# A four-layer graph network on one core: first transfers spread over three queues, constants behind them, two layers started beside the one before, one copy given priority

## The chip, the cores and the metric

The kernel runs on one core of one Trainium2 chip. The metric is the time of one execution in device microseconds (us); lower is better. Engines in the profile: PE is TensorE's matmul, DVE is VectorE, ACT is ScalarE, POOL is GpSimd, SP is SyncE, which here only issues transfers.

## The reference, cut to what matters

128 graphs of 64 nodes with 256 features go through four residual layers, each followed by a layer normalisation.

```python
# layer 0: five fixed groups of nodes, a two-step graph convolution each, mixed by softmax(fusion_w)
A = adj_g + eye;  dinv = deg(A) ** -0.5;  norm = dinv * A * dinv.T
h = relu(norm @ (x_g @ W1[g]) + b1[g]);   o = relu(norm @ (h @ W2[g]) + b2[g])
x = layernorm(x + scatter_add(softmax(fusion_w)[g] * o))
# layer 1: one graph convolution with the whole adjacency;  layer 2: a cubic in adj / rowsum, leaky relu
x = layernorm(x + norm(adj) @ (x @ W) + b)
x = layernorm(x + leaky(sum_k conv_w[k] * (adj/rowsum)**k @ (x @ W.T) + conv_b))
# layer 3: five GRU steps over messages from the neighbours
for l in range(5):
    h = gru_cell((adj != 0) @ (h @ weight[l]), h)
x = layernorm(x + h * mask)
```

All arithmetic is float32. The kernel does layer 0 in 8 batches of 16 graphs, layers 1 and 2 and the GRU in 16 chunks of 8 graphs.

## The kernel before

Layer 0 works through its batches with generators: `prep` makes the scaled adjacency of the next batch, `groups` multiplies this one, `residual` adds and normalises the last. Each engine gets its instructions in a fixed order. For TensorE in the later part that is the program's order; for the others a scheduler decides when the program is built.

```python
def load0(s):                        # one batch: 18 adjacency pieces, 12 x pieces, two whole x chunks
    ...
    nc.sync.dma_start(a0[s % 2][rows, t, col : col + m], adj[b, f : f + n, fc : fc + m])
    ...
    nc.sync.dma_start(xg[rows, t, :], x[b, f : f + n, :])
    ...
loaded = {0: load0(0)}
ident = const(c_ident, [128, 128], "ident", nc.scalar)
...
for g in range(NG):                  # ten weights of 512 KB
    nc.scalar.dma_start(W1[:, g], ...)
    nc.gpsimd.dma_start(W2[:, g], ...)
b2c = const(...);  fw = spread(fusion_w, NG, "fw", w0)
fm = ... ; fe = exp(...) ; gw = softmax ; gb2 = b2c * gw     # a chain over VectorE and ScalarE

def prep(s):
    nc.vector.tensor_add(ae, a, eye0)
    nc.vector.tensor_reduce(deg, ae, AX.X, ALU.add)
    dinv = inv_sqrt(deg, NT, TR, "d0")        # the power runs on GpSimd: d0s -> d0r -> d0o
    ...
    nc.tensor.transpose(p[:, t, :], A0[:, t0 + t, :], ident[:TR, :TR])
    nc.vector.tensor_mul(AT[:, t0 : t0 + n, :], p, dinv...)
    ...
for s in range(NS):                           # layer 0
    ...
    interleave(*beside, groups(s))
interleave(residual(NS - 1))                  # stores x1[c] to DRAM

loaded = {0: load(0), 1: load(1)}             # reloads x1 and the whole adjacency of two chunks
... # constants of layers 1 and 2
    interleave(both(mid(0), mid(1)), fold())  # layers 1 and 2 of two chunks, beside folding the GRU weights

def turn(self, k):                            # GRU: new state, transposed, copied for the next messages
    p = self.transpose(...)
    if not last:
        nc.scalar.copy(self.h[:, :, f], pv)
    ...
```

## Time and profile before

| what | before |
|---|---|
| time, median of 3 runs | 2423.56 us (2421.87 to 2425.59) |
| TensorE busy | 2270.2 us, 94% |
| to the first matmul | 38.68 us |
| batches 0 and 1, to batch 2's transposes | 67.08 us |
| from there to batch 7's transposes | 202.16 us |
| from there to the first GRU product | 176.79 us |
| GRU | 1939.89 us |

The last five rows cut the profiled run of 2424.6 us where the same work starts, so that they can be laid beside any other version. The page and the stretches are shown in the prediction below. One place that it mentions without showing is the start of layers 1 and 2 (TensorE's timeline: start, length, engine, line, operation, out<-in, shapes, count, then the idle time before it and what ended it):

```profile
396.51 1.09 PE L535 MATMUL pT<-ident,A 128*128 128x128 f32 x4 [19.78 <-DVE d1z L89]
...
404.45 3.78 PE L496 MATMUL pa<-AT,xt 128*128 128x128 f32 x16 [6.00 <-DVE AT L536]
```

TensorE stood still for 19.78 us and then, after eight transposes, for 6.00 more.

### The profile page before, as it was taken

The numbers are of one execution on the slowest core, as the hardware profiler recorded it, in microseconds if no ns is written. First come the engines' busy times: TensorE is split into PE (matmuls) and PEld (weight loads), VectorE is DVE, ScalarE is ACT, GpSimd is POOL, SyncE is SP. The second block draws the span as 40 slices with busy tenths as digits, with TensorE's granted clock in tenths as the row PEclk, the third lists the DMA queues.
The fourth block names the chain that finished last, engine by engine and source line by source line (L and its number), as shares of the span: only waits on it lengthen the run. The fifth ranks groups of instructions, "written<-read, shape, count | busy, mean of one in ns | idle before, by whom it ended". The sixth has DMA issues, their size and how long they took to land.

```text
span 2424.6 us, 31697 instructions
## 1 busy us (share of the span) xinstructions
PE 2270.2 (94%) x12288; PEld 2001.0 (83%) x12288; DVE 1324.7 (55%) x2914; ACT 1094.5 (45%) x2102; POOL 569.4 (23%) x606
## 2 busy tenths in 40 slices
PE   3999994899999999999999999999999999999996
PEld 2778783788888888888888888888888888888885
DVE  1334324555566556655666566656665566556556
ACT  1343441445454545454445444444544454445443
POOL 1101002222222322222222213222322232223221
PEclk9999997999999999999999999999999999999998
DMA  5232113000001000100010001000100000000000
GB/s 152 67 86 85 50 53 117 3 3 1 3 6 33 1 3 1 38 1 3 1 38 1 3 1 38 1 3 1 36 2 1 1 27 1 1 1 18 1 1 18
DMA packets 55319, 54.34 MB, mean 22 GB/s; under 512 B 24225, under 2 KB 48513, under 8 KB 55169
## 3 DMA queue, kind: packets, MB, share of 16 engines
q1 hardware_dynamic: 51616, 43.74, 5.8%
q0 software_dynamic: 1504, 5.51, 0.7%
q10 hardware_dynamic: 2048, 3.06, 0.4%
q8 instruction: 97, 1.59, 0.3%
q14 instruction: 54, 0.43, 0.1%
HBM read 35.52 MB, written 16.78 MB: 22 GB/s over the span
## 4 chain that ended last, share of the span: by engine, by line
PE 78%; DVE 13%; ACT 4%; DMA 2%; issue 2%; POOL 1%; SPq 1%; POOLq 0%; ACTq 0%; DVEq 0%
PE parz L460 19%; PE pan L460 9%; PE pdrz L460 9%; PE pa L496 8%; PE ps L289 5%; PE pdn L460 5%; PE pbrz L460 5%; PE ph L274 4%; PE pT L596 3%; PE pbn L460 3%; PE pd L575 2%; ACT xt L113 2%; DMA a<-in_adj_dram 2%; PE pp L550 1%; DVE st L102 1%
## 5 line engine op out<-in xcount | busy, mean ns | idle before, releaser
L476 ACT COPY c<-parz 128x512 f32<-128x512 f32 x240 | 140.4, 585 | 362.7 <-PE parz L460 362.7
L460 PE MATMUL parz<-Th,WHH 128*128 128x256 f32 x960 | 285.9, 379 | 0.0
L460 PE MATMUL parz<-Ta,V 128*128 128x256 f32 x960 | 285.5, 379 | 0.0
L440 POOL TENSOR_TENSOR Th<-hn 128x512 f32<-128x512 f32 x64 | 93.5, 1461 | 659.7 <-DVE hn L656 659.7
L653 ACT ACTIVATE NI<-NI,bih 128x512 f32<-128x512 f32 x160 | 115.5, 722 | 227.0 <-DVE NI L649 227.0
L460 PEld LDWEIGHTS parz<-Ta,V 128*128 128x128 f32 x960 | 182.4, 190 | 24.8
L476 ACT COPY c<-pan 128x512 f32<-128x512 f32 x240 | 140.8, 586 | 122.2 <-PE pan L460 122.2
L460 PEld LDWEIGHTS parz<-Th,WHH 128*128 128x128 f32 x960 | 176.0, 190 | 21.2 <-ACT c L476 0.5
L440 POOL TENSOR_TENSOR Ta<-agg 128x512 f32<-128x512 f32 x80 | 101.6, 1270 | 369.9 <-ACT agg L499 369.9
L488 DVE TENSOR_TENSOR RZ<-pdrz,c 128x512 f32<-128x512 f32 x80 | 55.2, 690 | 223.0 <-PE pdrz L460 223.0
L626 ACT ACTIVATE RZ<-RZ,brz 128x512 f32<-128x512 f32 x160 | 106.9, 716 | 121.3 <-DVE RZ L488 121.3
L107 POOL TENSOR_TENSOR rs<-ve,mhalf 128x4 f32<-128x4 f32 x64 | 64.6, 1010 | 408.6 <-DVE ve L105 396.3
L496 PEld LDWEIGHTS pa<-A,h 128*128 128x128 f32 x1024 | 128.1, 198 | 33.0 <-ACT h L669 30.4
L496 PE MATMUL pa<-A,h 128*128 128x128 f32 x1024 | 131.6, 284 | 24.8 <-ACT h L669 24.8
L460 PE MATMUL pan<-Ta,V 128*128 128x256 f32 x480 | 143.2, 380 | 3.1 <-ACT c L476 3.1
L482 DVE TENSOR_TENSOR NI<-pbn,c 128x512 f32<-128x512 f32 x80 | 55.3, 691 | 164.0 <-PE pbn L460 163.9
L460 PE MATMUL pan<-Th,WHH 128*128 128x256 f32 x480 | 142.8, 379 | 0.0
L289 PE MATMUL ps<-W,hg 128*100 128x256 f32 (+3 forms) x576 | 133.2, 384 | 0.0
L113 ACT ACTIVATE xt<-xt,nb,rs 128x256 f32<-128x256 f32 x192 | 99.6, 589 | 43.9 <-DVE nb L110 43.6
L289 PEld LDWEIGHTS ps<-W,hg 128*100 128x100 f32 (+3 forms) x576 | 91.8, 164 | 27.8
L478 DVE TENSOR_TENSOR NI<-pdn,c 128x512 f32<-128x512 f32 x80 | 54.8, 684 | 104.8 <-ACT c L476 104.8
L655 DVE TENSOR_TENSOR RZ<-RZ 128x512 f32<-128x512 f32 x160 | 109.8, 686 | 2.3
(183 smaller groups left out, 5241.1 us busy)
## 6 DMA issues: line engine op xcount, KB each, us to landing
xt<-in_x_dram SPq DMA_DIRECT2D x16, 512.0 KB
x<-xt SPq DMA_DIRECT2D x16, 512.0 KB
xt<-x SPq DMA_DIRECT2D x16, 512.0 KB
out_dram<-xt SPq DMA_DIRECT2D x16, 512.0 KB
xg<-in_x_dram SPq DMA_DIRECT2D x32, 100.0 KB
W<-in_w_dram POOLq DMA_DIRECT2D x5, 512.0 KB, 9.2
W<-in_w_dram ACTq DMA_DIRECT2D x5, 512.0 KB
a<-in_adj_dram SPq DMA_DIRECT2D x16, 128.0 KB
```

The lines of the kernel that those rows point to most:

```text
L107: nc.gpsimd.tensor_tensor(rs, ve, mhalf[:, :NP], ALU.pow)
L113: nc.scalar.activation(y[:, p, :], y[:, p, :], AF.Identity, bias=nb[:, p : p + 1], scale=rs[:, p : p + 1])
L274: nc.tensor.matmul(p, W1[:, g, k, e * 128 : (e + 1) * 128], ag0[:, k, o : o + w], start=k == 0, stop=k == 1)
L289: nc.tensor.matmul(p[:r, h, :], hg[:, e, TOFF[t] - o : TOFF[t] - o + r], W2[:, g, e, :], start=e == 0, stop=e == 3,)
L440: nc.gpsimd.tensor_sub(t[:, 0:2, :], a[:, :, H:], a[:, 0, :].rearrange("p (s n) -> p s n", s=2))
L460: nc.tensor.matmul(bank[:, g, :], w[:, q, i - 1, :], rhs, start=i in (1, 2, 5) and g == 0 and m == 0, stop=m == len(side) - 1, skip_group_ ...
L476: nc.scalar.copy(c, self.a)
L496: nc.tensor.matmul(p[:, q * 128 : (q + 1) * 128], src[:, q, k * 128 : (k + 1) * 128], m[:, q, :], start=True, stop=True)
L596: nc.tensor.transpose(p[:, q * 128 : (q + 1) * 128], src(q, k), ident)
L626: nc.scalar.activation(RZ[:, q, 0, :], RZ[:, q, 0, :], AF.Sigmoid, bias=b[0])
L653: nc.scalar.activation(n, n, AF.Tanh, bias=bih[:, 4 + j : 5 + j])
L655: nc.vector.tensor_mul(d, d, z)
```

## The change

The intent is to fill TensorE's idle stretches: get the first batches' data in first, load what the middle needs during layer 0, give TensorE two chunks of layers 1 and 2 beside layer 0's last batch, and let the copy that the GRU's messages wait for pass other work on ScalarE. The diff, cut to its core (moved code and names are left out, and the pools: layer 0's eight PSUM buffers, a pool of its own before, are now shared with the later layers, as five and three, and the tiles of layers 1 and 2 no longer come from a pool opened after layer 0):

```diff
 def load0(s):
+    qa = [nc.scalar, nc.sync] if s == 0 else [nc.sync]      # adjacency pieces
+    qx = nc.gpsimd if s < 2 else nc.sync                     # x pieces
...
-loaded = {0: load0(0)}
-ident, eye0, block0, b1 on ScalarE;  W1 on ScalarE, W2 on GpSimd;  b2, fw on SyncE
+eye0 = const(c_eye0, [TR, NT, NJ], "eye0", nc.scalar, w0)
+packed = {0: load0(0)}
+ident, block0, b1 on ScalarE;  W1, W2 on SyncE
+packed[1] = load0(1)
+xts = {0: load_x(0)}
+b2c = const(..., "b2", nc.scalar, w0)
+fw = spread(fusion_w, NG, "fw", w0, nc.scalar)
...
 for s in range(NS):
-        beside.append(prep(s + 1))
+        beside.append(prep(s + 1) if s else both(range(6), prep(s + 1)))   # batch 1: six steps later
+    if s == 1:          # constants of layers 1 and 2, on GpSimd behind its latest power
+    elif s == 3:        # GRU weights, the same way
+    elif s == NS - 1:
+        for c in (0, 1):
+            loaded[c] = load(c)
+        beside.append(both(mid(0), mid(1)))
     interleave(*beside, groups(s))
...
-    interleave(both(mid(0), mid(1)), fold())
+    weights = fold()    # now in three parts, around the two chunks' states and messages
...
     if not last:
-        nc.scalar.copy(self.h[:, :, f], pv)
+        with tc.high_priority():
+            nc.scalar.copy(self.h[:, :, f], pv)
```

## The prediction

> **What bounds the kernel now.** I read the page's first part, then the busy time by stretch, the chain of waits at the start and in the middle, TensorE's timeline at both, and last who TensorE waits for in the long GRU part.
>
> ```profile
> PE 2270.2 (94%) x12288; PEld 2001.0 (83%) x12288; DVE 1324.7 (55%) x2914; ACT 1094.5 (45%) x2102; POOL 569.4 (23%) x606
> ...
> PE   3999994899999999999999999999999999999996
> ```
>
> TensorE is the bound at 94%; VectorE is next at 55%. So the time can fall only where a slice of TensorE isn't 9: the first, slices 7 and 8, and the last, which is the tail of the final chunk. Cutting the run at the program's stages (columns: start:end, length, then PE busy with its count and the other engines', granted clock, DMA share, GB/s):
>
> ```profile
> 0.00:38.60 38.60, 0.00 (x0) 0.00 (x0) 2.84 (x11) 0.00 (x0) 8.63 (x12) 1.00 0.66 198
> 38.60:97.50 58.90, 52.46 (x286) 44.10 (x287) 12.80 (x53) 20.58 (x46) 3.60 (x2) 0.94 0.26 65
> 97.50:340.00 242.50, 235.20 (x1495) 196.85 (x1494) 86.98 (x315) 101.67 (x240) 21.10 (x17) 1.00 0.22 71
> 340.00:484.70 144.70, 104.01 (x559) 89.53 (x558) 71.59 (x233) 45.89 (x122) 32.69 (x44) 0.85 0.16 58
> 484.70:2424.60 1939.90, 1878.52 (x9954) 1670.52 (x9952) 1150.54 (x2304) 926.39 (x1694) 503.35 (x532) 0.99 0.03 9
> ```
>
> Idle is 38.6 us before the first matmul, 6 in batch 0, 7 in batches 1 to 6, 41 (and a clock of 0.85) from the last batch of layer 0 to the first GRU matmul, 61 in the GRU. The start, from the chain of waits (start, length, what):
>
> ```profile
> 3.69 14.87 DMA a<-in_adj_dram
> 18.58 5.88 DMA a<-in_adj_dram
> ...
> 32.10 1.87 DMA a<-in_adj_dram
> ...
> 35.51 1.84 POOL d0r L93
> ```
>
> The adjacency pieces sit in one queue with the x pieces and stand still for 15 us, while ten weight transfers of 512 KB fill the wires (up to 350 GB/s in that stretch). Batch 0 then waits again, for batch 1's adjacency, and is left at the lower clock; TensorE's timeline:
>
> ```profile
> 38.68 1.90 PE L239 MATMUL pT<-ident,A 112*112 112x112 f32 x9 [38.68 <-DVE A L219]
> ...
> 62.38 1.90 PE L239 MATMUL pT<-ident,A 112*112 112x112 f32 x9 [5.14 <-DVE A L219]
> 64.07 9.19 PE L289 MATMUL ps<-W,hg 128*100 128x256 f32 x32
> ...
> 96.65 1.07 PE L336 MATMUL pse<-ident,fusedT 128*128 128x128 f32 x8 [1.18 <-DVE fusedT L319]
> ```
>
> In the GRU, TensorE's waits (total us, times, longest):
>
> ```profile
> PE pa L496 <- ACT h L669: 24.8, 14, 2.0
> PE pp L550 <- DVE poly L552: 12.2, 14, 0.9
> ```
>
> One of those 14 on ScalarE and on TensorE:
>
> ```profile
> 546.16 2.07 ACT L113 ACTIVATE xt<-xt,nb,rs 128x256 f32<-128x256 f32 x4 [0.67 <-DVE nb L110]
> 548.14 0.81 ACT L624 ACTIVATE RZ<-parz,brz 128x256 f32<-128x256 f32 x2
> 548.86 0.57 ACT L669 COPY h<-pT 128x512 f32<-128x512 f32 x1
> ...
> 549.48 3.67 PE L496 MATMUL pa<-A,h 128*128 128x128 f32 x16 [1.89 <-ACT h L669]
> ```
>
> The copy was ready at 545.0 but stood behind four normalisations and two sigmoids; the gather then took 3.67 us in place of its usual 1.95.
>
> **What the Trainium skill says.** "TensorE: Matmul & The Clock Gate", Part 1: the array's clock is halved unless it has been busy for a window of about 3.4 us. The trace agrees: nine transposes take 1.90 us after an idle stretch and 1.03 us in running batches, and 32 `ps` matmuls take 9.19 us at 64.07 and 7.07 us at 308.79. So a removed long wait pays some 1 to 4 us more than its length. "DMA: Bandwidth & Descriptors", Issuing engines are not separate DMA queues: other queues share the same 16 DMA engines and save only issue time. The trace agrees: adjacency on SyncE's queue starved although the weights came from ScalarE's and GpSimd's. So the reordering of weights behind the first batch should matter more than the third queue. "GPSIMD Engine Reference", Instruction dispatch: the first call of a freshly loaded kernel may cost about 6 us that no profile line shows. No run here shows it yet: GpSimd had 28 us to spare before its first power.
>
> **The change, part by part.** I also compared the built order of instructions of both kernels.
>
> *Start.* Eighteen adjacency pieces go nine each to SyncE and ScalarE: 9 x 0.65 us an issue, behind one 512 KB weight, so landed by about 11 us; degree and power operand ready by 12. But GpSimd now issues 24 x pieces (batches 0 and 1) before its first power: at the 0.75 us an issue of today's weight issues, 18 us, plus two memsets of 0.94 and 1.82, plus some waits because only eight of its transfers are in flight by the program's semaphores: 21 to 24 us, power done at 24 to 26 (30 to 32 if the 6 us come on top). The first matmul follows the power by 38.68 - 37.34 = 1.3 us. I take 27.5 in place of 38.68: 11 gained. The weights (4.7 MB behind the adjacency, at 300 GB/s 16 us) land by 28 and batch 1's adjacency by about 45; the built order moves batch 1's transposes from behind the first hidden product (19 us into batch 0) to about 38 us into it, so the 5.1 us wait and its half clock (2.1 + 0.9) should go: 8 gained. Start: 19.
>
> *Layer 0's boundaries.* At six of seven, two `ph` matmuls now stand ahead of the `pse` that waited 1.18 us; they cover 0.67. Gain 4.
>
> *Middle.* Full-clock TensorE work in the stretch of 144.7 us: the last batch 35 (36.4 from 340.15 to its end, less the wait); layers 1 and 2 of two chunks, each 0.87 + 1.78 + 1.82 + 3.45 + 1.78 + 3.45 = 13.1 by durations in the GRU part, 26; 120 weight-folding matmuls at 14.02/64 = 0.219, 26; states and gathers of two chunks 6. Sum 93, so at most 51 can be gained. Today the store of x1, its reload, the adjacency and the GRU weights lie in between; all of these are now loaded during layer 0. What stays is a chain: after each layer 1 product VectorE adds, adds the bias (1.22), takes statistics (2.5), GpSimd takes a power (1.0), ScalarE normalises: 7 to 8.5 us. The built order covers about 5 of it for the first chunk and 2.4 for the second: 3 + 6 us of stalls, and 2 for the clock. The last `pse` waits for additions queued behind the second chunk's layer 2 (4). The third folding product can't be copied out until VectorE has finished the last residual, about 12 us (4 to 6 of stall). Small ones 3. About 23 stay; gain 28.
>
> *GRU.* The copy now stands ahead of the two sigmoids and of two of the four normalisations (seven times) or one (seven times). At 546.16 it would start at 547.2, end at 547.75; TensorE is there at 547.43: 0.4 us left of 1.89. For the other seven 1.8 us comes off, nearly all. So 24.8 becomes about 3: 22, and 0.2 to 0.5 each for the clock, 4. What is pushed back (half a normalisation, sigmoids with slack) should cost 1. Gain 25.
>
> Sum 19 + 4 + 28 + 25 = 76: 2424 - 76 = 2348.
>
> **Rivals.** (1) GpSimd becomes the start's bound: the loading cost, slow descriptor writing or landings of 9.2 us (the median of its weight transfers today) push the power to 33 or more. Then the start gives only 8 and the time is about 2359. For it: all x pieces and the power share one engine. Against: its issues today run back to back. (2) Layers 1 and 2 beside the last batch stall in order: TensorE executes in a fixed order, so every late normalisation also holds layer 0's matmuls, and the fold waits at its end for VectorE. The middle then gives 12 and the time is about 2364. For it: the chain above; against: VectorE is busy only half of the stretch. (3) The state copy's wait just moves to `pp`, or to a copy out of a gate bank: the GRU gives 8, time 2365. Against: the sigmoids have no waiter on TensorE in the wait list. All three together: about 2392. In the other direction, no stalls in the middle and a first matmul at 20 us give about 2320.
>
> **Range and chances.** The parts are nearly independent, with errors of about 7, 2, 10 and 6 us; together 14, and I lean slightly to the slow side for what a fixed order does: 2322 to 2376. The 2% line is 2375. Faster by over 2%: 0.88; within: 0.12; slower: nothing in it adds TensorE work.
>
> **What would show it.** First transposes near 27.5 and no wait of 5 us for batch 1; the first GRU matmul near 484.7 - 51 = 434, at a clock above 0.95 in that stretch; waits on the state copy under 6 us in total; the GRU part 1915 us long instead of 1940. Wrong if GpSimd's last x issue ends after 25 us, if the stretch from the last batch's first hidden product to the first gate product is longer than 130 us, or if another wait of 10 us or more appears in the GRU list.

## The result

After: 2358.25 us (median of 4 runs, 2355.82 to 2359.72); before, on the same chip in the same rounds, 2424.57 (2421.87 to 2428.22). The ratio is 0.9725, with a 95% interval of 0.9708 to 0.9741. Ratios here are the mean time of one kernel's runs over that of the other's of the same rounds, so they are not quite the ratio of the medians quoted. The kernel is faster by 2.7%; the time is inside the predicted range and 10 us above the predicted number. All outputs are right.

The page of after, its TensorE row by busy time and its 40 slices:

```profile
PE 2263.4 (96%) x12288; PEld 1999.1 (85%) x12288; DVE 1329.6 (56%) x2914; ACT 1092.8 (46%) x2102; POOL 584.9 (25%) x631
...
PE   4989998999999999999999999999999999999996
```

The dip in slices 7 and 8 has shrunk to one slice of 8; the first slice is still a 4, and slice 3 has become an 8 (the wait in batch 3 below). Cut at the same work as the table above (start:end, length, busy time with counts of PE, PEld, DVE, ACT and POOL, granted clock, DMA share, GB/s):

```profile
0.00:30.86 30.86, 0.00 (x0) 0.03 (x1) 3.71 (x16) 1.58 (x2) 18.98 (x31) 1.00 0.86 217
30.86:98.13 67.27, 64.44 (x326) 54.06 (x327) 17.37 (x69) 22.82 (x52) 8.29 (x9) 0.90 0.32 91
98.13:305.06 206.93, 198.32 (x1247) 165.45 (x1246) 79.78 (x296) 84.60 (x200) 29.60 (x27) 0.98 0.27 86
305.06:448.06 143.00, 131.37 (x768) 113.37 (x767) 76.65 (x229) 58.92 (x152) 32.13 (x40) 0.95 0.13 45
448.06:2356.50 1908.44, 1869.23 (x9953) 1666.23 (x9951) 1152.10 (x2308) 924.85 (x1696) 495.85 (x524) 1.00 0.03 9
```

| stretch | before | after | gained | predicted |
|---|---|---|---|---|
| to the first matmul | 38.68 | 30.86 | 7.8 | 11 |
| batches 0 and 1 | 67.08 | 67.27 | -0.2 | 8 |
| to batch 7's transposes | 202.16 | 206.93 | -4.8 | 4 |
| to the first GRU product | 176.79 | 143.00 | 33.8 | 28 |
| GRU | 1939.89 | 1908.44 | 31.5 | 25 |
| all | 2424.6 | 2356.5 | 68.1 | 76 |

So the sum hides two misses of opposite sign: layer 0 with its start gave 2.8 us in place of 23, and the rest gave 65.3 in place of 53.

**Where layer 0's gain went.** At the start, VectorE and GpSimd (the same columns as above, from two timelines):

```profile
17.37 0.17 DVE L96 TENSOR_TENSOR d0s<-deg,d0z 112x9 f32<-112x9 f32 x1
27.14 0.16 DVE L318 TENSOR_REDUCE fm<-fw 128x1 f32<-128x5 f32 x1 [9.60 <-DMA fw<-in_fusion_w_dram]
...
29.56 0.16 DVE L100 SCALAR_TENSOR_TENSOR d0o<-deg,d0r 112x9 f32<-112x9 f32 x1
```

```profile
23.22 1.83 POOL L98 TENSOR_TENSOR d0r<-d0s,mhalf 112x9 f32<-112x9 f32 x1
```

The power was done at 23.22 + 1.83 = 25.05 us, in the predicted 24 to 26. But the instruction that takes its result, `d0o`, stands in VectorE's order behind the softmax of the fusion weights, and those 2.5 KB were the last entry in ScalarE's queue. They were issued at 13.24 us and landed 13.88 us later. The first matmul came 5.8 us after the power in place of 1.3.

In batch 0, TensorE and then VectorE:

```profile
71.90 3.71 PE L380 MATMUL pa<-AT,xg 100*128 100x100 f32 x16 [2.82 <-issue]
```

```profile
67.93 0.39 DVE L340 TENSOR_TENSOR ae<-a,eye 112x225 f32<-112x225 f32 x1 [12.58 <-DMA a<-in_adj_dram]
...
71.10 0.17 DVE L100 SCALAR_TENSOR_TENSOR d0o<-deg,d0r 112x9 f32<-112x9 f32 x1 [1.94 <-POOL d0r L98]
71.19 1.33 DVE L369 TENSOR_TENSOR AT<-pT,d0o 112x448 f32<-112x448 f32 x3
```

The wait "issue" has no releaser in the profile, so VectorE's list has to tell it. TensorE wants batch 1's `AT` (71.19). Its transposes were done at 68.2, but in VectorE's order the first addition of batch 2 (67.93) stands ahead of it, with the degree chain that hangs on it. The addition waited for an adjacency which SyncE issued from 43.71 us on, behind everything else. That came just before the transposes were done; what held `AT` after them was the rest of batch 2's chain, and most of that was GpSimd's power, for which VectorE stood 1.94 us at `d0o`. TensorE then ran at half clock for 13 us, although it was never idle in them (stretches, columns as above):

```profile
72.00:79.00 7.00, 7.00 (x34) 7.00 (x34) 3.29 (x15) 2.00 (x5) 0.00 (x0) 0.50 0.09 9
79.00:85.00 6.00, 6.00 (x26) 5.43 (x25) 0.00 (x0) 1.40 (x3) 0.00 (x0) 0.50 0.01 2
86.00:90.00 4.00, 4.00 (x24) 3.23 (x23) 0.91 (x4) 2.38 (x7) 0.00 (x0) 1.00 0.42 128
```

In batch 3, TensorE and VectorE once more:

```profile
175.99 1.94 PE L464 MATMUL pse<-ident,fusedT 128*128 128x128 f32 x8 [7.25 <-DVE fusedT L448]
```

```profile
174.22 0.42 DVE L182 TENSOR_REDUCE rsum<-a 128x4 f32<-128x256 f32 x1 [8.56 <-DMA a<-in_adj_dram]
```

That is the same pattern a third time. The scheduler had pulled the row sum of the third chunk, which layer 1 needs much later, in front of two additions of layer 0, and its adjacency was late. In none of these three places did the data of TensorE's own operand come late; what stood ahead of it on VectorE did.

**The middle.** What is left there (TensorE):

```profile
365.39 0.71 PE L159 MATMUL pa<-poly,xt 128*128 128x128 f32 x4 [1.13 <-ACT xt L118]
...
393.77 1.23 PE L159 MATMUL pa<-poly,xt 128*128 128x128 f32 x4 [4.33 <-ACT xt L118]
...
408.53 2.50 PE L464 MATMUL pse<-ident,fusedT 128*128 128x128 f32 x16 [3.45 <-DVE fusedT L448]
...
426.14 8.86 PE L549 MATMUL pf<-ih,wl 128*128 128x256 f32 x32 [2.14 <-ACT w L556]
```

The waits of 19.78 and 6.00 us are gone. Two waits for normalised chunks, one for VectorE's additions and one for a copied weight stay, 11.05 us in sum.

**The GRU.** The waits of TensorE in that part (total us, times, longest):

```profile
PE pp L214 <- DVE poly L216: 12.2, 14, 0.9
...
PE pa L159 <- ACT h L697: 3.2, 11, 0.4
```

The wait for the state copy fell from 24.8 to 3.2 us, and no other took its place: `pp` stands at 12.2 as before.

### The profile page after: what moved, and what is told of

The parts are those of the page before. It is cut to its first block, busy times and chain, and to the rows that moved or that the text cites. A ratio compares the mean times of both kernels' runs of the same rounds, so it can differ in the third digit from the quotient of the medians.

```text
span 2356.5 us, 31696 instructions
## 1 busy us (share of the span) xinstructions
PE 2263.4 (96%) x12288; PEld 1999.1 (85%) x12288; DVE 1329.6 (56%) x2914; ACT 1092.8 (46%) x2102; POOL 584.9 (25%) x631
## 4 chain that ended last, share of the span: by engine, by line
PE 82%; DVE 11%; ACT 2%; issue 2%; DMA 1%; POOL 1%; SPq 0%; ACTq 0%; POOLq 0%; DVEq 0%
PE parz L583 20%; PE pan L583 10%; PE pdrz L583 10%; PE pa L159 8%; PE pdn L583 5%; PE pbrz L583 5%; PE ps L418 5%; PE ph L403 4%; PE pT L623 3%; PE pbn L583 3%; PE pd L239 2%; PE pa L380 2%; ACT xt L118 1%; PE pp L214 1%; DVE st L107 1%
## 5 line engine op out<-in xcount | busy, mean ns | idle before, releaser
L159 PE MATMUL pa<-A,h 128*128 128x128 f32 x1024 | 125.8, 277 | 3.2 <-ACT h L697 3.2
L118 ACT ACTIVATE xt<-xt,nb,rs 128x256 f32<-128x256 f32 x192 | 101.2, 591 | 34.1 <-DVE nb L115 33.8
L403 PE MATMUL ph<-ag,W 128*128 128x96 f32 (+3 forms) x640 | 114.2, 333 | 0.0
```

Of the source, the lines that this page charges most:

```text
L118: nc.scalar.activation(y[:, p, :], y[:, p, :], AF.Identity, bias=nb[:, p : p + 1], scale=rs[:, p : p + 1])
L159: nc.tensor.matmul(p[:, q * 128 : (q + 1) * 128], src[:, q, k * 128 : (k + 1) * 128], m[:, q, :], start=True, stop=True)
L403: nc.tensor.matmul(p, W1[:, g, k, e * 128 : (e + 1) * 128], ag0[:, k, o : o + w], start=k == 0, stop=k == 1)
```

## The experiments

My theory after reading the two traces: the copy's priority is worth 31 us by itself; the early loads are most of the middle; and layer 0's missing 20 us are three waits in VectorE's order, each of which can be taken away alone. Rivals: the GRU gain needs the rest of the change; the place beside the last batch makes the middle; GpSimd or the three queues bound the start. Twelve kernels ran. Times are medians of 4 or 5 runs. They ran in four groups, each on another chip. The kernel before ran in each, with medians from 2423.25 to 2426.03 us, and the ratios are against it; the changed kernel ("after") ran in none of them. So a difference from it, or between versions of two groups, is sure only to about 3 us.

**prio_only: the copy's priority alone, on the kernel before.**

```diff
+                with tc.high_priority():
+                    nc.scalar.copy(self.h[:, :, f], pv)
```

> The kernel before with the priority of the state copy alone. If the GRU gain is the copy alone: TensorE's waits on it fall from 24.8 us to about 3, the GRU part from 1940 to about 1908 us, the time by 31 us to 2393 (2389 to 2398). If only the wait is the copy's and the rest came with other parts of the change (the new tiles, the longer run at full clock ahead of it): 22 us, 2402. If the copy is nothing without the rest: 2424.

Measured: 2396.83 us against 2424.36, ratio 0.9893 (0.9862 to 0.9924). The trace is clearer than the time, whose runs spread from 2395.68 to 2405.88. The GRU part is 1908.5 us long and the waits on the copy are 3.2 us, both as in the changed kernel. The priority alone does it all.

**no_prio: the changed kernel without it.**

```diff
-                with tc.high_priority():
-                    nc.scalar.copy(self.h[:, :, f], pv)
+                nc.scalar.copy(self.h[:, :, f], pv)
```

> The changed kernel with the priority of the state copy taken away. If the copy is worth the same here as alone: the GRU part is back at about 1940 us, the time 2389 (2385 to 2394). If other parts of the change carry some of the GRU gain: 2368 to 2380.

Measured: 2388.5 us, ratio 0.9847 (0.9827 to 0.9867). The waits on the copy are back at 24.9 us and the GRU part is 1936.1 us long: 30.3 us lost in time, 27.7 in the GRU part of the profiled run. The 3.8 us by which that part is still shorter than before are clock: TensorE's busy time in it is 1875.0 in place of 1878.5 us and its idle time is the same. Runs of one kernel differ by as much (the kernel before by 11.6 us beside these runs), so nothing is read from them.

**mids_after: all the early loads, but layers 1 and 2 after layer 0.**

```diff
-                beside.append(both(mid(0), mid(1)))
...
+        interleave(both(mid(0), mid(1)), fold())
```

> The changed kernel with all its early loads, but with layers 1 and 2 of the first two chunks run after layer 0 and interleaved with the weight folding, as in the kernel before. If the loads are most of the middle's gain (the wait of 19.78 us and the 6.0 us that follow it were for the reloaded chunk and the folding weights): only some 5 us are lost, 2363 (2360 to 2367). If the place beside the last batch is the gain: 15 us or more are lost, 2374 or more.

Measured: 2367.24 us, ratio 0.9759 (0.9739 to 0.9779): 9 us lost, just above my theory's range and between the two theories. From batch 7's transposes to the first GRU product it takes 153.5 us, against 176.8 before and 143.0 after. So the early loads give 23.3 us of the middle's 33.8 and the place beside the last batch 10.5. Each has company that was not tested alone: the new pools stay in this run with the loads, and the folding, which the change cuts into three parts, is in one piece again with the place. I had put the second at 5. The wait for `AT`, 6.00 us before, is 6.70 here although all loads are early, and I had counted it with the loads. It is a wait for VectorE: in its list layer 0's last additions and statistics run from 371.5 us to 379.5, and `AT` comes at 379.64.

**w_front: three queues, but the weights in front again.**

```diff
+            nc.scalar.dma_start(W1[:, g], ...)     # ahead of the adjacency
+            nc.gpsimd.dma_start(W2[:, g], ...)     # ahead of the x pieces
```

> The changed kernel with the ten weight transfers of 512 KB back in front of the first batch's pieces, on ScalarE's and GpSimd's queues; the pieces stay on their three queues. If the order of the transfers is what matters: the first matmul at 38 us or later instead of 30.9, the time 2366 or more. If the three queues are: the first matmul below 33 us and the time 2358 to 2361.

Measured: 2366.73 us, ratio 0.976 (0.9739 to 0.978). The first matmul comes at 45.56 us, 14.7 later than after and even 6.9 later than before. The order of the transfers matters, as the theory had it. Part of the 45.56 is the softmax again: the power was done at 35.95 + 1.83 = 37.78, and `d0o` ran at 44.26, behind fusion weights that landed at 41.8. The clean measure of the order is the power, 12.7 us later than after's 25.05. The time lost, 8.5 us, is a sum with luck in it. Batches 0 and 1 lost another 7.8 us, to a wait of 10.31 us behind a row sum of the middle, which came to stand in batch 0 here (VectorE):

```profile
90.02 0.42 DVE L182 TENSOR_REDUCE rsum<-a 128x4 f32<-128x256 f32 x1 [22.70 <-DMA a<-in_adj_dram]
```

The stretch to batch 7's transposes, without its 7.25 us wait, was 9.9 us shorter, and the middle 3.2.

**fw_first: the fusion weights first on ScalarE's queue.**

```diff
+        fw = spread(fusion_w, NG, "fw", w0, nc.scalar)
         eye0 = const(c_eye0, [TR, NT, NJ], "eye0", nc.scalar, w0)
...
-        fw = spread(fusion_w, NG, "fw", w0, nc.scalar)
```

> The changed kernel with the fusion weights (2.5 KB) first on ScalarE's queue instead of last, so that the softmax no longer stands in VectorE's order in front of the first degree scaling with a wait for it. Theory: the first matmul follows the power (25.05 us) by 1.3, so comes at about 26.4 instead of 30.9, and the time falls by 4 to 2354 (2352 to 2356). Rival: GpSimd or the layer 0 weights bound the start at nearly the same time, or batch 0 gives it back: first matmul at 29 or later, or time 2357 to 2359.

Measured: 2359.78 us, ratio 0.9735 (0.9721 to 0.9748): nothing gained, the rival's outcome (its range ended at 2359). Two things came of it. The softmax chain ends with a product with the second bias, which I had left late in the queue; it landed at 27.67 us and held VectorE in the same place, so the first matmul came at 29.06. And batch 0 gave back the 1.8 us and more: its wait grew from 2.82 to 8.05 us, because batch 2's adjacency came no earlier but 2.3 us later (its addition ran at 70.21 in place of 67.93). The edit was too small to test the step; small_first below does it.

**at_first: batch 2's first addition queued behind batch 1's last `AT`.**

```diff
-            nc.vector.tensor_add(ae, a, eye0)
+            with tc.issue_after(lastAT[-1].ins):     # same engine, order only
+                nc.vector.tensor_add(ae, a, eye0)
```

> The changed kernel with batch 2's first addition queued behind batch 1's last transposed adjacency on VectorE. Theory: the wait of 2.82 us at 71.9 us, and the half clock of the next 11 us, are this order's: they go, 7 us, 2351 (2349 to 2354). Rival: batch 1's transposes or gathers wait for something else, or the wait comes back a batch later, when batch 2's adjacency is late: 2356 to 2359.

Measured: 2347.42 us, ratio 0.9683 (0.967 to 0.9696), 10.8 us faster than after and below my range. Batches 0 and 1 take 57.9 us instead of 67.3: 9.4 gained by a wait of 2.82 us, the rest of it clock. Another 1.2 are an earlier first matmul (29.64), which the edit was not meant to move. The wait in batch 3 went too, but an equal one came in batch 2. TensorE and VectorE of this run:

```profile
132.69 2.29 PE L408 MATMUL ph<-ag,W 128*128 128x144 f32 x8 [7.80 <-DVE xt L473]
```

```profile
131.35 0.69 DVE L174 TENSOR_TENSOR Ab<-a,pair 128x512 f32<-128x512 f32 x1 [12.68 <-DMA a<-in_adj_dram]
```

Here the first chunk's masked adjacency for layer 1 stands ahead of batch 1's residual. A small edit rearranges the scheduler's whole order; which instruction of the middle gets in the way is chance, but in most of these builds one does.

**rsum_late: the row sums of chunks 2 and later queued behind layer 0's last normalisation.**

```diff
-        nc.vector.tensor_reduce(rsum, a64, AX.X, ALU.add)
+        with ExitStack() as late:
+            if c >= 2:
+                late.enter_context(tc.issue_after(norms[-1].ins))
+            nc.vector.tensor_reduce(rsum, a64, AX.X, ALU.add)
```

> The changed kernel with the row sums of chunks 2 and later queued behind layer 0's last normalisation on VectorE. Theory: the wait of 7.25 us at 176 us is the third chunk's row sum standing in front of two additions with a wait for a late adjacency; it goes, with the clock that it cost, 8 us, 2350 (2348 to 2353). Rival: the additions were waiting for ScalarE's z all the same: at most 2 us, 2356 to 2358.

Measured: 2350.89 us, ratio 0.9697 (0.9684 to 0.9711). The stretch from batch 2's to batch 7's transposes takes 197.0 us instead of 206.9 and the wait of 7.25 us is gone. That is 9.9 us. A start and batches 0 and 1 that came out longer by 0.7 and 1.0, and a middle longer by 2.4, against 1.0 gained in the GRU, leave 6.8 between the profiled runs (2356.5 - 2349.7). The additions had not been waiting for ScalarE.

**one_queue: all pieces of batches 0 and 1 on SyncE, the weights still behind batch 0.**

```diff
-            qa = [nc.scalar, nc.sync] if s == 0 else [nc.sync]
-            qx = nc.gpsimd if s < 2 else nc.sync
+            qa = [nc.sync]
+            qx = nc.sync
```

> The changed kernel with all pieces of batches 0 and 1 on SyncE's queue, the weights still behind batch 0 there. Theory, that the order does it and a queue saves only issue time: 30 issues at 0.65 us end at about 20 us, the power is done at 24 to 26, and the fusion weights, early on ScalarE's now nearly empty queue, hold nothing: first matmul at 26 to 30, but the weights end later, at about 38, and batch 1's pieces too, so batch 0 gets some waits: 2355 to 2363. Rival, that the three queues do it: first matmul at 35 or later, 2364 or more.

Measured: 2346.9 us, ratio 0.9686 (0.967 to 0.9703). One queue is better than three by 11 us, beyond my range. First matmul at 26.50 us, which is 4.4 of the 11; 30 issues had ended at 21.1 us; the fusion weights, early on a nearly empty queue, held nobody. Waits of 5.21 us (88.77) and 3.65 us (141.57) came up, and the 7.25 us of batch 3 are not there. What it does not show is that three queues are bad as such: with one queue the small constants come early, GpSimd is free for its power, and batch 1's transposes come to stand where no late addition is ahead of them. Three queues with the small constants in front and at_first's edit (small_first, next) take the same time.

**small_first: both small constants of the softmax chain first, with at_first's edit.**

```diff
+        fw = spread(fusion_w, NG, "fw", w0, nc.scalar)
+        b2c = const(..., "b2", nc.scalar, w0)
         eye0 = const(c_eye0, [TR, NT, NJ], "eye0", nc.scalar, w0)
```

> The changed kernel with both small constants of the softmax chain (fusion weights 2.5 KB, second bias 5 KB) first on ScalarE's queue, together with the edit of at_first. The run fw_first moved only the fusion weights, and the product with the second bias then waited until 27.67 us in the same place in VectorE's order. Theory: with both in front the first matmul follows the power (25 to 27 us) by 1.3 us, at 26.5 to 28, and with batch 0's wait gone the start is kept: time 2345 (2343 to 2347), against 2347.4 of at_first. Rival: the power itself is put off further, because GpSimd's own x transfers hold it: first matmul at 29 or later, time 2347 or more.

Measured: 2346.42 us, ratio 0.9678 (0.9663 to 0.9694). VectorE and TensorE at the start:

```profile
25.30 0.17 DVE L100 SCALAR_TENSOR_TENSOR d0o<-deg,d0r 112x9 f32<-112x9 f32 x1 [5.10 <-POOL d0r L98]
```

```profile
26.61 1.90 PE L373 MATMUL pT<-ident,A 112*112 112x112 f32 x9 [26.61 <-DVE A L353]
```

VectorE now waits for the power and for nothing else, and the first matmul follows it (23.43 + 1.84 = 25.27) by 1.3 us, as the prediction had it. The start is 3.0 us shorter than at_first's, while the time is lower by only 1.0, which runs on two chips cannot tell from nothing. The profile, of the slowest of the four runs (2350.22 us), has another wait of 4.00 us at 81 us, which probably took most of it: VectorE had stood 8.47 us at `cI`, a product for layer 2, for four constants that SyncE issued late. No run takes that wait away alone.

**queues_by_use: a version built from these results.** Batch 0's adjacency alone on SyncE, its x pieces on ScalarE, small constants first, x pieces of batches 1 and 2 on GpSimd behind a power, with the edits of at_first and rsum_late.

```diff
+                    if s not in (1, 2):
+                        (nc.sync if s else nc.scalar).dma_start(*pieces.pop())
...
+            elif s == 2:
+                with tc.issue_after(powers[-1].ins):
+                    for p in pieces:
+                        nc.gpsimd.dma_start(*p)
```

> Built from what the runs so far show: batch 0's adjacency alone in front on SyncE, its x pieces on ScalarE behind the constants, no transfer on GpSimd ahead of the first power; x pieces of batches 1 and 2 on GpSimd behind the power of the batch ahead; the edits of at_first and rsum_late. Theory: 18 adjacency issues end at about 13 us, power done at 17 to 19, first matmul at 19 to 21 instead of 26.5 (all on one queue), no wait of 5 us for batch 2, the 7.25 us of batch 3 gone: 2346.9 - 6 - 5 - 8 = 2328 (2324 to 2335). Rival: the weights behind the adjacency become the bound of batch 0 as soon as it starts earlier (they landed at about 30 us in all runs): first products wait, 2336 to 2342.

Measured: 2342.59 us, ratio 0.9659 (0.9645 to 0.9674), just above the rival's range, and not for its reason. The weights held nothing. The first matmul came at 24.83 instead of 19 to 21, because 18 adjacency issues took 17.40 us while ScalarE issued 12 x pieces in the same time; and the first chunk's masked adjacency got in front of a residual, 11.14 us on VectorE and 4.31 on TensorE at 134.5.

**mid_a_batch_earlier: the same, with the first chunk's layers 1 and 2 one batch earlier.**

```diff
-            elif s == NS - 1:
-                for c in (0, 1):
-                    loaded[c] = load(c)
-                beside.append(both(mid(0), mid(1)))
+            elif s >= NS - 2:
+                c = s - NS + 2
+                loaded[c] = load(c)
+                beside.append(mid(c))
```

> The kernel queues_by_use, with layers 1 and 2 of the first chunk beside the last batch but one, and those of the second chunk alone beside the last batch. Theory, that what stays in the middle are the normalisation chains of two chunks packed beside one batch of 36 us: the waits of 1.1 and 4.3 us for normalised chunks shrink to 1 or 2, minus 4 us. Rival: the normalisations are not covered better, and the last batch's own waits (3.45 us for VectorE's additions, 2.14 us for the copied weights) stay: within 1.5 us of queues_by_use.

Measured: 2348.59 us, ratio 0.9684 (0.9669 to 0.97): 6 us slower, which neither side expected. The waits for normalised chunks did shrink, from 1.13 and 3.65 to 0.68 and 1.16 us. But a new wait of 8.09 us at 302 us came up, for the reload of the first chunk. SyncE stores a later chunk at 296.05, waits 2.2 us for that store to land, and only then issues the reload, at 298.67. The likely reason is that the reload takes the buffer of that chunk, of which there are five; that reason is argued only (counted in the program, the reload takes the 17th of these buffers' tiles and the chunk just stored, batch 5's second, has the 12th: they share a buffer if the five go round in order), and what the placement would be worth without the wait is open.

**single_then_gpsimd: the last version.** Batch 0's adjacency first and its x pieces behind it, both on SyncE alone; every chunk's masked adjacency and row sum queued behind the latest normalisation; the rest as in queues_by_use.

```diff
+            if s == 0:
+                for p in pieces:
+                    nc.sync.dma_start(*p)
...
+        with tc.issue_after(norms[-1].ins):
+            nc.vector.tensor_mul(Ab..., a64..., pair...)
...
+        with tc.issue_after(norms[-1].ins):
+            nc.vector.tensor_reduce(rsum, a64, AX.X, ALU.add)
```

> Last version: batch 0's adjacency first and its x pieces behind it, both on SyncE alone (in queues_by_use two queues at once made 18 adjacency issues take 17.4 us, one queue had made 30 issues take 20.4); both small constants first on ScalarE; x pieces of batches 1 and 2 on GpSimd behind a power; batch 2's addition behind batch 1's last transposed adjacency; every chunk's masked adjacency and row sum in layers 1 and 2 queued behind the latest normalisation of layer 0, because in queues_by_use the first chunk's masked adjacency held VectorE for 11.1 us and TensorE for 4.31 us. Theory: first matmul at 19 to 21 us in place of 24.8, the products behind it at about 23, no wait over 2 us until layer 0's last batch: 2342.6 - 3 - 6 = 2333 (2329 to 2338). Rival: the x pieces or the weights, which now leave later, hold the first products or batch 0: 2339 to 2345.

Measured: 2331.36 us (2329.77 to 2332.99, 5 runs), ratio 0.9618 (0.9605 to 0.9631). It beats both kernels: 92 us under before, 27 under after. First matmul and SyncE's issues (start, length, queue, line, what, count), and for comparison SyncE's half of the same 18 issues in the changed kernel:

```profile
20.45 1.90 PE L389 MATMUL pT<-ident,A 112*112 112x112 f32 x9 [20.45 <-DMA xg<-in_x_dram]
```

```profile
1.65 12.93 SPq L289 DMA_DIRECT2D a<-in_adj_dram  x18
```

```profile
1.24 11.20 SPq L286 DMA_DIRECT2D a<-in_adj_dram  x9
```

The profile puts the first matmul's wait down to a transfer of x, which a transpose of `A` does not read. It follows the power (17.30 + 1.81 = 19.11) by 1.3 us as before, so the power is what it waited for; the x transfer landed at the same moment. The parts of this version were not tested apart.

The largest waits left before the last batch are 2.18 us at 82 and 1.19 at 232.

## Why the prediction was right or wrong

The total came within 10 us because a miss of 20 in layer 0 was met by 12 more than predicted in the rest: that is luck. Of the signs that the prediction named, the waits on the copy (3.2 us) and the length of the GRU (1908) came true; the first transposes (30.86 in place of 27.5) and the first GRU product (448.06 in place of 434) did not, and the clock in that stretch was 0.94 in place of above 0.95 (340.00 to 448.06 us). None of its signs of being wrong appeared: GpSimd's last x issue ended at 21.4 us, the stretch from the last batch's first hidden product took 110.8 us, and no new wait of 10 us came up in the GRU.

**GRU: mechanism right, one term too small.** "So 24.8 becomes about 3: 22" was measured as 24.8 to 3.2, and prio_only and no_prio show that it is the copy. The mis-sized term is the clock, "0.2 to 0.5 each for the clock, 4". TensorE's busy time in the part fell by 1878.51 - 1869.23 = 9.3 us, and the "1" for what is pushed back did not show. 22.2 less idle and 9.3 less busy make the 31.5. The prediction's reading "the time can fall only where a slice of TensorE isn't 9" is wrong for this part: all its slices but the last showed 9, and a 9 hides up to a tenth of idle time and any loss of clock.

**Middle: mechanism right, pessimistic.** Predicted 28, measured 33.8. Of the stalls that I expected to stay, the normalisation chains cost 1.13 + 4.33 = 5.5 in place of 9, the wait of the last `pse` 3.45 in place of 4, the folding product 2.14 in place of 4 to 6. mids_after shows 23.3 of the gain to be the loads and 10.5 the place beside the last batch. Rival (2) of the prediction, stalls that leave only 12, is refuted.

**First matmul: the failing step is "The first matmul follows the power by 38.68 - 37.34 = 1.3 us".** The power came when predicted; in the kernel before, the softmax stands behind the first transposes in VectorE's order, and in the changed one in front of `d0o`, behind a transfer that lands last. I had compared both built orders and looked there for TensorE's and GpSimd's instructions, not for what VectorE has in front of `d0o`. With the constants in front it is 1.3 again (small_first), at 26.61 us, where 27.5 had been predicted. The prediction's Rival (1), GpSimd, is half right: it had the right place and the wrong engine. The step before it failed as well, without cost here: "9 x 0.65 us an issue [...] landed by about 11". Nine issues took 11.20 us on SyncE and 9.62 on ScalarE, so the degree's operand was ready at 17.5, not 12. GpSimd's own issues, which end at 21.4, hid it.

**Batch 0: the failing step is "the 5.1 us wait and its half clock (2.1 + 0.9) should go: 8 gained".** The wait for batch 1's adjacency went. A wait of 2.82 us for batch 2's took its place through VectorE's order, with 13 us of half clock behind it. Without it the gain is 67.08 - 57.85 = 9.2 (at_first).

**Boundaries: "Gain 4" is right for what it looked at.** Of seven waits of 1.18 us, one is left, at 256.86. The stretch got longer all the same, by the 7.25 us wait for the third chunk's row sum. Without that it is 202.2 - 197.0 = 5.1 shorter (rsum_late).

So all three terms of layer 0 were about the right size, and each was eaten by the same thing, which the sum had no term for: an in-order engine that is only half busy, with an instruction in front whose transfer is late (in batch 0 with a power on GpSimd hanging on it). The prediction names TensorE's fixed order as a risk (Rival 2) and takes VectorE's 55% as slack. Half of its time being free is no slack for the instruction behind such a wait. The Trainium skill says it in "TensorE: Matmul & The Clock Gate", Part 2, Step-by-step: what each phase is for: "PE is the *only* engine that reorders", and that only for weight loads. The trace agrees: `d0o` was executable at 25.05 and ran at 29.56.

"So the reordering of weights behind the first batch should matter more than the third queue" held more strongly than I meant: w_front undoes the order and starts at 45.56, one_queue undoes the queues and starts at 26.50.

## What to carry to other kernels

When transfers are pulled ahead, read for every engine that feeds the bound one what stands in front of the awaited instruction in its built order, and when that one's data lands: two transfers of 2.5 and 5 KB at the end of a queue put the first matmul off by 4 us here, and single instructions of a later layer cost 7 to 8 us of waiting. Pin such instructions behind the work that must not wait: one such edge gained 9.4 us where it acted, nearly as much as undoing two additional queues did in all. A copy that the bound engine waits for is worth its priority many times over when it recurs 14 times, and the clock it saves comes on top.

## What the Trainium skill lacked or had wrong

- "TensorE: Matmul & The Clock Gate", Part 1, What's actually happening: it gives about 3.4 us of sustained work as enough to return to the full clock. In batch 0 of the changed kernel the clock stayed at 0.50 for 13 us (72 to 85 us) with TensorE busy in all of them, after an idle time of only 2.82 us; after the wait of 7.25 us in batch 3 it was back about 5 us after work began. So a wait cost between 2.7 us more than its length (9.9 for 7.25, rsum_late) and 6.6 more (9.4 for 2.82, at_first). The start is the same in every version: after a long idle time, in the last version, nine transposes take 1.90 us in place of a later batch's 1.03, 36 `pa` 7.98 in place of 1.93 + 2.38, and 32 `ph` 8.78 in place of 7.34 (before, at 97.72). That is half speed for about 12 us, an estimate from these durations, and some 6 us that no version here won back; the clock column reads 1.00 there, so durations have to tell it. What decides the length is open.
- "DMA: Bandwidth & Descriptors", Issuing engines are not separate DMA queues: it says that further issuing engines save the time of issuing. Between SyncE and ScalarE they hardly saved that here: 18 adjacency pieces took 12.93 us on SyncE alone, and 11.20 us split nine and nine over SyncE and ScalarE with GpSimd issuing beside them; beside ScalarE's 12 x pieces the 18 took 17.40. GpSimd's issues did save it: the changed kernel had all 30 pieces of batch 0 issued by 12.4 us, 12 of them from GpSimd by 10.15, where one queue took until 21.1 (one_queue). No page has an issue time for several engines at once.
- "GPSIMD Engine Reference", Instruction dispatch: the 6 us of a first call did not show in these profiled executions. In the last version the operand was written at 17.05 + 0.17 = 17.22 us, the first power ran from 17.30 and took 1.81 us, as later ones do (1.80). Whether this program loads such a kernel at all, no run shows.
- No page has it, or none that I found: waits that the profile puts down to "issue" (2.82 us in the changed kernel, 8.05 in fw_first, 10.31 in w_front) were waits for another engine's result all the same; only that engine's timeline shows it.
